# A macaron block (FFN, attention, FFN): the FFNs' down products by one level of Strassen's scheme, with sums on GpSimd and a new order of steps

## The chip, the cores and the metric

The kernel runs on one core of one Trainium2 chip. The metric is the device time of one execution in microseconds (us). Engines are named as in the profile: PE is TensorE (PEld its weight loads), DVE is VectorE, ACT is ScalarE, POOL is GpSimd, SP is SyncE, which issues most DMAs. Each engine works through its own queue in program order; semaphores carry what one engine needs of another.

## What is computed

Eight samples of 512 tokens with 256 channels pass through three residual branches. All of it is float32.

```python
x = x + 0.5 * ffn(layernorm(x))      # f1
x = x + attention(layernorm(x))      # at: 16 heads, causal, 32 wide
x = x + 0.5 * ffn(layernorm(x))      # f2, same weights as f1
def ffn(x):
    h = butterfly(x @ W_exp + b_exp, up_weights)     # 256 -> 1024, ten stages
    h = gelu(h + up_bias)
    return butterfly(h, down_weights) @ W_con + b_con + down_bias   # 1024 -> 256
```

The butterflies are linear, so the kernel folds each into its dense matrix once, at the start: an up matrix of 256 x 1024 (`wup_sb`) and a down matrix of 1024 x 256 (`wdn_sb`). The down product of one FFN of one sample is then a matrix of 512 x 1024 (gelu's output `g`) times one of 1024 x 256. There are sixteen of them.

## The kernel before

**The fold** (lines 719 to 742) builds the two matrices on all engines. For the down matrix, `high_stage` runs three times; its half on POOL is line 250, its sums on DVE are line 253. Between the stages the gelu steps of the first sample's f1 are issued. `low_down` (lines 342 to 346) finishes with eight products on PE (line 345) and eight copies on ACT into `wdn_sb` (line 346). After it stand the bias that `ffn_bias` (line 200, POOL) adds to x, and the layernorm of the next sample's f1.

**The steps.** Everything else is cut into steps of about 1.7 us on PE, and `ORDER` (lines 636 to 669) writes out by hand, sample by sample, in which order they are issued to all the queues. A token is a count, a letter and a distance to the sample that is meant. `f` and `g` are up steps of f1 and f2 (line 378): 128 of the 1024 hidden features for all 512 tokens, then gelu on ACT (line 392). `F` and `G` are down steps (line 396). `q`, `v`, `w` are the attention's projections. `u0` to `u9` are score units: products into the four banks `sc` (line 492), mask and maximum on DVE (line 506), exponentials on ACT (line 519). `t` transposes probabilities on DVE (line 537), `m` sends them across partitions by DMA (line 563), `p` multiplies them with v (line 576) and scales (line 583). `s`, `a`, `x` are a layernorm's statistics, application and transposition; the statistics use POOL for a power (line 169), the application is DVE's line 183, the transposition goes through DRAM by DMA except in three places.

**Products.** `product` (line 349) writes 128 output partitions as four matmuls of 32 columns of weights each, which run side by side in the array. In the profile each appears as two matmuls with two weight loads, as float32 needs two passes. I call the four that start together a burst.

**A down product** has eight steps: for each of four blocks of 128 tokens, twice four of the eight blocks of hidden features. Weights are 32 columns of `g`, and the 256 channels of `wdn_sb` are streamed:

```python
for fc in range(half * NBLK // 2, (half + 1) * NBLK // 2):
    product(py[:, i, :], lhsT=g[:, fc, bass.ts(t, P)], rhs=wdn_sb[:, fc, :],
            start=(fc == 0), stop=(fc == NBLK - 1))
```

Two token blocks share one bank of PSUM, and one DVE instruction adds them to x (line 414). For f2 SP then writes them to DRAM (line 416). In the last sample each block is added and written alone.

**Memory of PSUM.** Three banks (`ps_a`) turn over among up, down and projection products; four hold `sc`; one (`ps_o`) is for `p`.

Of the kernel before, what the change touches and what calls it, by code (L numbers as in the profile page):

```python
# [42 lines left out]
P = 128  # L43
# [5 lines left out]
def macaron_kernel(  # L49
# [64 lines left out]
    wdn_sb = const.tile([P, NBLK, C], F32, name="wdn_sb")  # L114

# [60 lines left out]
    def ln_apply(b, what, half, engine=nc.vector):  # L176
# [9 lines left out]
        if by_dma(b, what):  # L186
            if half == 0:
                kept["tx", what, b] = lnp.tile([P, 4, KC, NT, 32], F32, name=f"tx_{what}_{b}", tag="tx", bufs=2)
            for t in range(2):
                nc.vector.transpose(  # L190
                    kept["tx", what, b][:, :, :, 2 * half + t, :].rearrange("p j k r -> p k j r"),
                    xn[:, t, :].rearrange("p (k j s) -> p k j s", k=KC, j=4),
                )
# [94 lines left out]
    def first_ln_transposes():  # L288

        pts = [ps_f.tile([P, 512], F32, name=f"pxt_f1_0_{kc}", tag="f") for kc in range(KC)]  # L290
        xnt = kept["xnt", "f1", 0] = work.tile([P, 4, KC, P], F32, name="xnt_f1_0", tag="xnt", bufs=3)
# [57 lines left out]
    def product(out, lhsT, rhs, start, stop):  # L349

        for c in range(0, P, 32):
            nc.tensor.matmul(out[c : c + 32], lhsT=lhsT[:, c : c + 32], rhs=rhs, start=start, stop=stop)  # L352

    def ln_steps(b, what, **how):
        def new():
            kept["xnt", what, b] = work.tile([P, 4, KC, P], F32, name=f"xnt_{what}_{b}", tag="xnt", bufs=3)
            return kept["xnt", what, b]
# [19 lines left out]

    def up_steps(b, what):
        def step(fc):
            if fc == 0:  # L380
                kept["g", what, b] = work.tile([P, NBLK, N], F32, name=f"g_{what}_{b}", tag="g")
            g, xnt = kept["g", what, b], kept["xnt", what, b]
# [9 lines left out]
            nc.scalar.activation(g[:, fc, :], ph[:, :N], AF.Gelu, bias=bup_sb[:, fc : fc + 1])  # L392

        return [partial(step, fc) for fc in range(NBLK)]

    def down_steps(b, what, store):
        def step(t, half):
            t2, i = divmod(t, 2)

            n = 1 if store and b == B - 1 else 2  # L400
            if i % n == 0 and half == 0:
                kept["py", what, b] = ps_a.tile([P, 512], F32, name=f"py_{what}_{b}_{t // n}", tag="a")
            g, py = kept["g", what, b], kept["py", what, b].rearrange("p (t c) -> p t c", c=C)
            for fc in range(half * NBLK // 2, (half + 1) * NBLK // 2):
                product(
                    py[:, i, :],
                    lhsT=g[:, fc, bass.ts(t, P)],
                    rhs=wdn_sb[:, fc, :],
                    start=(fc == 0),
                    stop=(fc == NBLK - 1),  # L410
                )
            if (i + 1) % n == 0 and half == 1:
                mine = xt[b][:, t + 1 - n : t + 1, :]
                nc.vector.scalar_tensor_tensor(mine, py[:, i + 1 - n : i + 1, :], 0.5, mine, ALU.mult, ALU.add)  # L414
                if store:
                    nc.sync.dma_start(
                        out=out[b, bass.ds((t + 1 - n) * P, n * P), :].rearrange("(t p) c -> p t c", p=P), in_=mine
                    )

        return [partial(step, t, half) for t in range(NT) for half in range(2)]  # L420

    def qk_steps(b):
        def step(which, g):
            w, scale = ((wq_sb, QSCALE), (wk_sb, 1.0))[which]
            dst = work.tile([P, N], F32, name=f"{'qk'[which]}t_{b}_{g}", tag=f"{'qk'[which]}t", bufs=6)
# [139 lines left out]
    def times_v(b, g, pool):  # L565
# [4 lines left out]
        pa = ps_o.tile([P, 512], F32, name=f"pa_{b}_{g}", tag="pa")  # L570
# [46 lines left out]
    def attention_steps(b, pool):  # L617
        def moved(g):
            turn_sums(b, g)
            move(b, g, pool)  # L620

        return {
            "u": lambda n: score_unit(b, *UNITS[n], pool),
            "t": lambda n, part=0: turn(b, *UNITS[n], part, pool),
            "m": moved,
            "p": lambda g: times_v(b, g, pool),
        }

    ORDER = {
        0: """7F+0 x1+1 sa+0 aa+0 F+0 sa+0 x1+1 2f+1 aa+0 xa+0 f+1 xa+0 f+1 s1+2 2q+0 f+1 s1+2 u0 a1+2 2q+0 u1 v
              q+0 v t0 t1b u2 v 2f+1 t1a f+1 t2a m0 a1+2 u3 t2b 2F+1 u4 x1+2 t3 2F+1 t4b sa+1 v x1+2 q+0 t4a F+1
              u5 p0 m1 t5 u6 3F+1 aa+1 sa+1 2q+0 u7 f+2 t6b aa+1 t6a f+2 xa+1 f+2 xa+1 u8 t7a p1 2f+2 m2 2f+2 t8
              f+2 q+1 t7b q+1 u9 q+1 t9a t9b 2q+1 p2 m3""",  # L640
        1: """u0 F+1 q+0 u1 2F+1 t0 u2 F+1 t1b 2q+0 t1a u3 t2a p-3 m0 u4 2w-1 s2-1 a2-1 w-1 v w-1 s2-1 v t2b a2-1
              F+1 u5 v t3 x2-1 sa+1 3F+1 t4b v x2-1 aa+1 u6 p0 2g-1 sa+1 s1+2 aa+1 t4a xa+1 m1 g-1 a1+2 t5 g-1
              s1+2 4g-1 G-1 u7 xa+1 G-1 a1+2 x1+2 t7a x1+2 4G-1 t6a t6b u8 p1 m2 u9 t8 2G-1 f+2 q+1 f+2 t7b t9b
              f+2 q+1 f+2 t9a f+2 q+1 p2 f+2 m3""",
        2: """u0 2q+0 u1 t0 q+0 2f+1 u2 2q+0 t1a u3 p-3 t2a t1b u4 m0 2w-1 F+1 t2b u5 F+1 t3 F+1 t4a w-1 t4b F+1
              l+2 s2-1 w-1 2v s2-1 v 2a2-1 v F+1 sa+1 x2-1 F+1 u6 p0 F+1 t6a x2-1 m1 F+1 t6b t5 aa+1 sa+1 aa+1
              xa+1 7g-1 u7 s1+2 g-1 G-1 u8 t7a p1 t7b xa+1 m2 a1+2 u9 2G-1 q+1 G-1 s1+2 a1+2 t8 t9b 3G-1 x1+2 G-1
              t9a q+1 x1+2 2q+1 p2 m3""",
        3: """u0 2q+0 l+2 f+1 t0 4f+1 u1 2f+1 u2 p-3 w-1 t1b w-1 s2-1 q+0 t2a t1a u3 t2b m0 v 2w-1 v u4 t3 q+0
              a2-1 v f+1 u5 s2-1 a2-1 t4b v t4a 4F+1 u6 p0 x2-1 F+1 x2-1 m1 sa+1 2F+1 s1+2 u7 F+1 sa+1 aa+1 4g-1  # L650
              t7a aa+1 t5 t6a 2g-1 t6b xa+1 u8 p1 g-1 xa+1 g-1 m2 t7b u9 q+1 s1+2 q+1 a1+2 G-1 t9a a1+2 x1+2 t8
              t9b 2G-1 q+1 x1+2 G-1 q+1 p2 m3""",
        4: """u0 3G-2 t0 q+0 u1 G-2 q+0 u2 t1b 2f+1 q+0 t1a u3 p-3 l+2 u4 w-1 t3 v w-1 f+1 t2a w-1 s2-1 m0 v w-1
              t4b s2-1 2f+1 t2b 2a2-1 q+0 f+1 v x2-1 f+1 2s1+2 f+1 2F+1 v u5 p0 u6 x2-1 F+1 t4a F+1 m1 F+1 u7 t6a
              3F+1 g-1 sa+1 t5 2g-1 aa+1 sa+1 aa+1 g-1 t7a 2g-1 t6b u8 p1 2xa+1 g-1 m2 a1+2 g-1 t8 G-1 u9 2G-1
              a1+2 q+1 t7b G-1 2x1+2 t9a 2q+1 G-1 q+1 t9b p2 m3""",
        5: """u0 3G-2 u1 q+0 t0 2q+0 u2 f+1 t1b 2f+1 t1a u3 p-3 u4 w-1 t2a v t2b w-1 s2-1 q+0 l+2 m0 f+1 s1+2 v t3
              v t4a f+1 u5 t4b a2-1 w-1 f+1 w-1 f+1 s2-1 a2-1 v x2-1 f+1 s1+2 F+1 u6 p0 x2-1 m1 t6b 2F+1 a1+2 u7
              3F+1 t5 a1+2 F+1 sa+1 F+1 g-1 t7a x1+2 sa+1 g-1 aa+1 2g-1 aa+1 u8 t6a xa+1 p1 xa+1 4g-1 m2 x1+2 u9
              t9b t8 2q+1 2G-1 q+1 G-1 t9a t7b G-1 p2 m3""",  # L660
        6: """u0 q+0 2G-2 u1 G-2 q+0 u2 G-2 t1a t1b 2f+1 t0 t2a 2f+1 u3 p-3 m0 u4 w-1 t2b w-1 v 2w-1 v s2-1 q+0 v
              t4b t4a v t3 s2-1 f+1 u5 p0 m1 2f+1 a2-1 t5 f+1 u6 q+0 a2-1 F+1 t6b q+0 F+1 u7 F+1 t6a F+1 x2-1 t7a
              p1 x2-1 t7b m2 u8 sa+1 3F+1 u9 F+1 2g-1 sa+1 aa+1 g-1 aa+1 g-1 xa+1 t9a g-1 t8 g-1 t9b p2 xa+1 2g-1
              2q+1 m3""",
        7: """q+0 u0 q+0 u1 2G-2 t0 u2 p-3 t1a w-1 t1b t2a G-2 m0 u3 w-1 G-2 s2-1 u4 v t2b v t4a t3 2w-1 t4b v
              s2-1 v p0 m1 q+0 2a2-1 q+0 u5 q+0 u6 t5 G-2 q+0 t6b u7 2x2-1 t6a G-2 t7a p1 m2 u8 2G-2 g-1 t8 2g-1
              u9 t9a 2g-1 l+1 g-1 t9b t7b p2 2g-1 2G-1 m3 3G-1 p3 2w+0 s2+0 2w+0 a2+0 s2+0 2G-1 a2+0 G-1 2x2+0 8g+0
              8G+0""",
    }
# [8 lines left out]
    def sequence(b, pool):  # L678
        for token in ORDER[b].split():
            times, rest = (int(token[0]), token[1:]) if token[0].isdigit() else (1, token)  # L680
            what, kind, at = rest[0], "", 0
            if what in "sax":
                kind, rest = rest[1], rest[1:]
            if what in "ut":
                part = "ab".find(rest[-1])
                n = int(rest[1]) if part >= 0 else int(rest[1:])
            elif len(rest) > 1:
                at = int(rest[1:])
            for _ in range(times):
                if what == "u":  # L690
                    attention_steps(b, pool)["u"](n)
                elif what == "t":
                    attention_steps(b, pool)["t"](n, max(part, 0))
                elif what == "m":
                    attention_steps(b, pool)["m"](at)
                elif what == "p":
# [143 lines left out]
```

## Time and profile before

| what | us |
|---|---|
| median of 3 runs | 872.11 (870.77 to 872.52) |
| the profiled execution | 870.19 |
| its span in the profile | 868.2 |
| PE busy in it | 847.7 |
| DVE, ACT, POOL busy | 629.4, 517.8, 92.2 |
| granted TensorE clock | 1.00 in every stretch |

The span runs from the first to the last instruction; 2.0 us of the execution lie around it. A group's row in the profile gives its line, engine and operation, output and inputs, shape and count, then its busy time and the mean duration of one instruction, then the idle time of the engine in front of it and what ended that. Matmuls overlap in the pipeline: the mean duration of one is several times what it adds to a stream.

### The profile page before, as it was taken

The page shows a single profiled execution, that of the slowest core. Times are in us where ns is not written, and L with a number is a line of the kernel's source. Part 1 is how long each engine was busy: PE and PEld are TensorE (multiplying, and loading weights), DVE is VectorE, ACT ScalarE, POOL GpSimd, SP SyncE. Part 2 cuts the span into 40 slices and gives each one's busy share as a digit, 9 for nine tenths or more (in the row PEclk, how much of TensorE's full clock was granted, in tenths as well). Part 3 has the DMA queues.
Part 4 walks back from the last instruction along what each step waited for, and adds up shares of the span by engine and source line. Part 5 has one row for each costly group of instructions (what it writes and reads, how often), then busy time and mean ns, then how long its engine had stood idle before and what let it go on. Part 6 is the DMA issues. An engine that isn't in the chain of part 4 may idle for free.

```text
span 868.2 us, 28463 instructions
## 1 busy us (share of the span) xinstructions
PE 847.7 (98%) x11914; PEld 370.1 (43%) x11914; DVE 629.4 (73%) x1815; ACT 517.8 (60%) x1359; POOL 92.2 (11%) x123
## 2 busy tenths in 40 slices
PE   8999999999999999999999999999999999989898
PEld 7443524444334443443443434335344343433454
DVE  7948985997579685699777585888567794977430
ACT  6618686654585474776585654865746764747210
POOL 6511000011001010010102010021000100010010
PEclk9999999999999999999999999999999999999999
DMA  9210766637656568267765277557684577367400
GB/s 334 70 50 18 206 183 153 159 110 204 179 135 159 146 175 225 54 178 189 195 172 135 83 192 193 134 140 202 166 188 123 127 190 200 99 174 198 129 14 26
DMA packets 52832, 130.41 MB, mean 150 GB/s; under 512 B 10849, under 2 KB 32609, under 8 KB 52705
## 3 DMA queue, kind: packets, MB, share of 16 engines
q1 hardware_dynamic: 52560, 128.57, 55.8%
q8 instruction: 94, 1.54, 0.8%
q14 instruction: 34, 0.27, 0.1%
q10 hardware_dynamic: 144, 0.02, 0.0%
HBM read 21.80 MB, written 15.20 MB: 43 GB/s over the span
## 4 chain that ended last, share of the span: by engine, by line
PE 80%; SPq 5%; DVE 5%; DMA 4%; ACT 3%; issue 1%; DVEq 0%; ACTq 0%
PE ph_f L352 22%; PE py_f L352 22%; PE pp L352 11%; PE sc L492 8%; PE po L352 6%; PE pv L352 6%; SPq L563 5%; PE pa L576 5%; DVE e L506 3%; DMA out_dram<-x 1%; ACT e L519 1%; DMA pt<-pr 1%; DVE pr L537 1%; DMA wexp_sb<-in_wexp_t_dram 1%; DMA x<-in_x_dram 1%
## 5 line engine op out<-in xcount | busy, mean ns | idle before, releaser
L519 ACT ACTIVATE e<-e,nm 128x128 f32<-128x128 f32 (+3 forms) x512 | 280.4, 549 | 93.6 <-DVE nm L506 93.2
L506 DVE CUSTOM_DVE_ANT_0 e<-sc,mask 128x384 f32<-128x384 f32 (+2 forms) x384 | 196.4, 552 | 98.4 <-PE sc L492 97.8
L352 PE MATMUL py_f<-wdn_sb,g_f 128*32 128x256 f32 x4096 | 232.4, 380 | 0.0
L352 PE MATMUL ph_f<-xnt_f,wup_sb 128*32 128x512 f32 x2048 | 228.6, 593 | 0.6 <-ACT g_f L392 0.3
L537 DVE STREAM_TRANSPOSE pr<-e 128x1536 f32<-128x1536 f32 (+2 forms) x128 | 171.2, 1356 | 19.8 <-ACT e L519 19.8
L352 PEld LDWEIGHTS py_f<-wdn_sb,g_f 128*32 128x32 f32 x4096 | 131.9, 110 | 100.2 <-issue 19.3
L392 ACT ACTIVATE g_f<-ph_f,bup_sb 128x512 f32<-128x512 f32 x128 | 84.7, 686 | 90.6 <-PE ph_f L352 90.1
L352 PEld LDWEIGHTS ph_f<-xnt_f,wup_sb 128*32 128x32 f32 x2048 | 65.2, 110 | 139.7 <-issue 113.7
L519 ACT ACTIVATION_READ_ACCUMULATOR e<-e,nm 128x1 f32 x512 | 96.0, 188 | 0.0
L492 PE MATMUL sc<-kt,qt 32*64 32x512 f32 (+5 forms) x2048 | 86.6, 431 | 6.9 <-DVE nm L506 4.9
L576 PE MATMUL pa<-pt,v 128*32 128x512 f32 (+3 forms) x1024 | 75.4, 435 | 5.3 <-DMA pt<-pr 3.5
L169 POOL TENSOR_TENSOR rstd_f<-mv_f,mhalf 128x2 f32<-128x2 f32 x32 | 22.4, 702 | 481.6 <-DVE mv_f L167 463.2
L492 PEld LDWEIGHTS sc<-kt,qt 32*64 32x64 f32 x2048 | 40.8, 130 | 61.2 <-issue 27.3
L352 PE MATMUL pp<-xnt_at,wq_sb 128*32 128x512 f32 x512 | 61.0, 594 | 0.0
L352 PE MATMUL pp<-xnt_at,wk_sb 128*32 128x512 f32 x512 | 61.0, 593 | 0.0
L352 PE MATMUL po<-wo_sb,ot 128*32 128x256 f32 x1024 | 59.7, 380 | 0.4 <-DVE ot L583 0.4
L352 PE MATMUL pv<-wv_sb,xnt_at 128*32 128x512 f32 x512 | 59.7, 593 | 0.0
L576 PEld LDWEIGHTS pa<-pt,v 128*32 128x32 f32 x1024 | 31.8, 109 | 60.6 <-issue 50.1
L414 DVE SCALAR_TENSOR_TENSOR x<-py_f,x 128x512 f32<-128x512 f32 (+1 forms) x34 | 22.1, 649 | 44.4 <-PE py_f L352 44.4
L200 POOL TENSOR_TENSOR x<-x,bhalf 128x512 f32<-128x512 f32 x32 | 41.0, 1283 | 120.4 <-DVE xn_f L183 117.4
L519 ACT ACT_TABLE_LOAD x28 | 35.9, 1283 | 23.9 <-DVE nm L506 23.7
L583 DVE TENSOR_TENSOR ot<-pa,pt 128x512 f32<-128x512 f32 x32 | 21.8, 680 | 35.8 <-PE pa L576 35.8
(89 smaller groups left out, 577.3 us busy)
## 6 DMA issues: line engine op xcount, KB each, us to landing
pt<-pr SPq DMA_DIRECT2D x508, 176.0 KB, 4.3
td_f<-tx_f SPq DMA_DIRECT2D x14, 512.0 KB, 4.5
xnt_f<-td_f SPq DMA_DIRECT2D x56, 128.0 KB, 2.9
x<-in_x_dram SPq DMA_DIRECT2D x8, 512.0 KB, 6.1
td_at<-tx_at SPq DMA_DIRECT2D x7, 512.0 KB, 2.6
xnt_at<-td_at SPq DMA_DIRECT2D x28, 128.0 KB, 3.0
out_dram<-x SPq DMA_DIRECT2D x14, 256.0 KB, 4.2
wexp_sb<-in_wexp_t_dram SPq DMA_DIRECT2D x2, 514.0 KB, 7.7
```

What stands on the lines that cost most here:

```text
L169: nc.gpsimd.tensor_tensor(rstd, mv[:, :, 1], mhalf, ALU.pow)
L200: nc.gpsimd.tensor_tensor(x2, x2, bhalf.rearrange("p (o c) -> p o c", o=1).to_broadcast([P, 2, C]), ALU.add)
L352: nc.tensor.matmul(out[c : c + 32], lhsT=lhsT[:, c : c + 32], rhs=rhs, start=start, stop=stop)
L392: nc.scalar.activation(g[:, fc, :], ph[:, :N], AF.Gelu, bias=bup_sb[:, fc : fc + 1])
L414: nc.vector.scalar_tensor_tensor(mine, py[:, i + 1 - n : i + 1, :], 0.5, mine, ALU.mult, ALU.add)
L492: nc.tensor.matmul(sc[s : s + ROWS, j, at + low : at + high], lhsT=kept["q", b, gg][r, bass.ds(qb * P + s, ROWS)], rhs=kept["k", b, gg][r, ...
L506: nc.vector.tensor_tensor_reduce(out=e[:, j, at : at + n], in0=sc[:, j, at : at + n], in1=mask[:, N - n :] if qb else mask_first, scale=-1 ...
L519: nc.scalar.activation(e[:, j, at : at + n], e[:, j, at : at + n], AF.Exp, scale=-1.0, bias=nm[:, qb, gg, j : j + 1], accum_out=zs[:, gg, ...
L537: nc.vector.transpose(pr[:, :, :, qb : qb + 3 * n - 2 : 3, :].rearrange("p j h k r -> p h k j r"), blocks[:, :, :n])
L563: nc.sync.dma_start(out=pt[bass.ts(j, 32), i], in_=pr[bass.ts(i, 32), j])
L576: nc.tensor.matmul(by_row[r, :, kb * 32 :], lhsT=v[:, kb, bass.ds(g * P + j * HD, HD)], rhs=pt[:, :, bass.ds(j * NSLOT + SLOT[kb] + kb, NT ...
L583: nc.vector.tensor_tensor(kept["ot", b][:, g, :].rearrange("p (i q r) -> p i q r", i=4, r=32), pa.rearrange("p (i q r) -> p i q r", i=4, r ...
```

## The change

The down product is cut into quarters, and seven products of quarters take the place of eight. Write the gelu output as a11, a12 (the first 256 tokens, with hidden features 0 to 511 and 512 to 1023), a21 and a22 (the other 256 tokens), and the down matrix as b11, b12, b21, b22 (hidden halves by channel halves). Weight sums are made once, in the fold, by four DVE instructions. Sums of `g` are made for every FFN on POOL, mostly in place. Seven steps k0 to k6 each multiply one pair and add the result to one or two quarters of x; since running sums stay in PSUM, the bank `u` collects k0, k3, k5 and k6, the bank `q` collects k2 and k4, and `r` holds k1. A step now has two token blocks times four feature blocks, and streams 128 channels per matmul.

```diff
+    wmix_sb = const.tile([P, 3, NBLK // 2, C // 2], F32, name="wmix_sb")
...
-                kept["tx", what, b] = lnp.tile([P, 4, KC, NT, 32], F32, name=f"tx_{what}_{b}", tag="tx", bufs=2)
+                kept["tx", what, b] = lnp.tile([P, 4, KC, NT, 32], F32, name=f"tx_{what}_{b}", tag="tx", bufs=1)
...
+    def mix_weights():
+        nc.vector.tensor_tensor(t1, b12, b11, ALU.subtract)
+        nc.vector.tensor_tensor(t2, b22, t1, ALU.subtract)
+        nc.vector.tensor_tensor(t4, b21, t2, ALU.subtract)
+        nc.vector.tensor_tensor(b12, b22, b12, ALU.subtract)
...
     def up_steps(b, what):
-        def step(fc):
+        def step(n):
+            pair, second = divmod(n, 2)
+            fc = pair + HALF * second
...
+            if second:
+                a11, a21, a22 = g[:, pair, EARLY], g[:, pair, LATE], g[:, fc, LATE]
+                nc.gpsimd.tensor_tensor(kept["s1", what, b][:, pair], a21, a22, ALU.add)
+                nc.gpsimd.tensor_tensor(a21, a11, a21, ALU.subtract)
...
+        def half_product(out, a, w, start):
+            for t in range(2):
+                for f in range(HALF):
+                    product(
+                        out[:, t, :],
+                        lhsT=a[:, f, bass.ts(t, P)],
+                        rhs=w[:, f, :],
+                        start=start and f == 0,
+                        stop=f == HALF - 1,
+                    )
...
+        def add(m, n, part, tokens=slice(0, 2)):
+            mine = quarter(m, n)[:, tokens]
+            nc.vector.scalar_tensor_tensor(mine, part[:, tokens], 0.5, mine, ALU.mult, ALU.add)
...
+            if k == 0:
+                kept["pu", what, b] = bank("u", ps_y, "y")
+                u = kept["pu", what, b][:, 0]
+                half_product(u, a11, w11, True)
+                for f in (slice(0, HALF // 2), slice(HALF // 2, HALF)):
+                    nc.gpsimd.tensor_tensor(a11[:, f], s1[:, f], a11[:, f], ALU.subtract)
+                add(0, 0, u)
+                return
...
+            if k == 1:
+                r = bank("r", ps_a, "a")[:, 0]
+                half_product(r, a12, w21, True)
+                for f in (slice(0, HALF // 2), slice(HALF // 2, HALF)):
+                    nc.gpsimd.tensor_tensor(a12[:, f], a12[:, f], a11[:, f], ALU.subtract)
+                add(0, 0, r)
+            elif k == 2:
+                kept["pq", what, b] = bank("q", ps_a, "a")[:, 0]
+                half_product(kept["pq", what, b], s1, t1, True)
+                add(1, 1, kept["pq", what, b])
+            elif k == 3:
+                half_product(u, a11, t2, False)
+                add(0, 1, u)
+            elif k == 4:
+                half_product(kept["pq", what, b], a12, w22, False)
+                add(0, 1, kept["pq", what, b])
+                put(0)
+            elif k == 5:
+                half_product(u, a21, t3, False)
+                add(1, 1, u)
+            else:
+                half_product(u, a22, t4, False)
+                add(1, 0, u)
+                put(1)
...
-        pa = ps_o.tile([P, 512], F32, name=f"pa_{b}_{g}", tag="pa")
+        pa = ps_a.tile([P, 512], F32, name=f"pa_{b}_{g}", tag="a")
...
         low_down(mats, cur)
+        mix_weights()
         run(partial(ffn_bias, 0, 0), partial(ffn_bias, 0, 1))
         run(lns(1, "f1"))
...
+    STEPS = """
+        2x1@1 5F@0 sa@0 F@0 aa@0 F@0 sa@0 2f@1 aa@0 2xa@0 s1@2 2q@0 f@1 u0@0 q@0 s1@2 t0a@0 a1@2 2f@1 q@0 u1@0
+        2v@0 a1@2 t1b@0 q@0 u2@0 t1a@0 3f@1 t2a@0 m0@0 u3@0 t2b@0 2F@1 u4@0 t3a@0 q@0 2F@1 v@0 t4a@0 2x1@2 u5@0
+        F@1 v@0 sa@1 t4b@0 p0@0 m1@0 u6@0 F@1 aa@1 t5a@0 2q@0 t6a@0 t6b@0 F@1 sa@1 2f@2 u7@0 2f@2 aa@1 u8@0 p1@0
+        2f@2 2xa@1 t7a@0 m2@0 f@2 u9@0 t8a@0 2q@1 t7b@0 t9a@0 f@2 F@2 q@1 u0@1 q@1 t9b@0 p2@0 m3@0 u1@1 F@2
...
+        xa@6 t7b@5 3g@4 m2@5 2g@4 G@4 u9@5 G@4 t8a@5 t9b@5 t9a@5 2q@6 2G@4 x1@7 q@6 p2@5 m3@5 G@4 u0@6 q@6 G@4
+        u1@6 G@4 t0a@6 2f@7 q@6 u2@6 t1b@6 f@7 p3@5 t2a@6 t1a@6 m0@6 2w@5 u3@6 t2b@6 v@6 q@6 u4@6 t4a@6 f@7 v@6
+        2w@5 u5@6 2v@6 t3a@6 t4b@6 p0@6 m1@6 t5a@6 3f@7 2s2@5 a2@5 f@7 u6@6 a2@5 2x2@5 2q@6 t6a@6 2F@7 t6b@6
...
+        w@6 s2@6 t3a@7 v@7 t4b@7 q@7 s2@6 2a2@6 t4a@7 2v@7 x2@6 v@7 p0@7 m1@7 u5@7 x2@6 q@7 G@5 u6@7 t5a@7 t6b@7
+        2G@5 q@7 u7@7 G@5 t6a@7 t7a@7 p1@7 m2@7 u8@7 G@5 t8a@7 5g@6 t7b@7 u9@7 g@6 t9a@7 g@6 t9b@7 p2@7 m3@7 g@6
+    """
```

`mix_weights` overwrites b12 with its difference from b22 (t3). The bank of `ps_o` becomes `ps_y` and holds `u`; `p` now takes a bank of `ps_a`. Up steps run in the order 0, 4, 1, 5, 2, 6, 3, 7, and after each second one POOL makes that pair's two sums. `STEPS` replaces `ORDER`: one list for all samples, in which the sample stands after `@`; steps f, g, q, v, w, u, t, m, p and the layernorms' are as numerous as before, F and G are seven per FFN. Of the list, the first four lines, three from late in it and the last two are shown. Three tags get fewer buffers: `tx` 1 in place of 2, `xnt` 2 in place of 3, `qt` and `kt` 5 in place of 6.

## The prediction

> **What bounds the kernel now.** I read the page's busy times first, then its chain of work that ended last.
>
> ```profile
> span 868.2 us, 28463 instructions
> PE 847.7 (98%) x11914; PEld 370.1 (43%) x11914; DVE 629.4 (73%) x1815; ACT 517.8 (60%) x1359; POOL 92.2 (11%) x123
> PE 80%; SPq 5%; DVE 5%; DMA 4%; ACT 3%; issue 1%; DVEq 0%; ACTq 0%
> ```
>
> PE is busy nearly throughout and is 80% of the chain. A busy PE proves little, as ends are modelled, so the waits on PE come next, together with those of its weight loads.
>
> ```profile
> PEld sc L492 <- DVE nm L506: 15.5, 19, 1.7
> PE sc L492 <- DVE nm L506: 4.9, 10, 0.8
> PE pa L576 <- DMA pt<-pr: 3.5, 2, 2.0
> ```
>
> The columns are us in total, times, longest. PE waits for little: 5 to 16 us on the score banks, 3.5 us on a transfer. So the length of PE's stream is the time, and what the change takes from that stream counts in full unless a new wait appears. Last I read groups with shapes kept apart, for prices.
>
> ```profile
> L352 PE MATMUL py_f<-wdn_sb,g_f 128*32 128x256 f32 x4096 | 232.4, 380 | 0.0
> L576 PE MATMUL pa<-pt,v 128*32 128x512 f32 x256 | 33.9, 601 | 5.3 <-DMA pt<-pr 3.5 <-DMA out_dram<-x 1.5 <-issue 0.3
> L576 PE MATMUL pa<-pt,v 128*32 128x256 f32 x256 | 19.8, 379 | 0.0
> L576 PE MATMUL pa<-pt,v 128*32 128x128 f32 x256 | 13.0, 273 | 0.0
> L329 PE MATMUL pup<-ident,high_up 128*128 128x128 f32 x8 | 1.0, 272 | 0.0
> L414 DVE SCALAR_TENSOR_TENSOR x<-py_f,x 128x512 f32<-128x512 f32 x30 | 20.4, 679 | 18.3 <-PE py_f L352 18.3
> L414 DVE SCALAR_TENSOR_TENSOR x<-py_f,x 128x256 f32<-128x256 f32 x4 | 1.7, 425 | 26.1 <-PE py_f L352 26.1
> L200 POOL TENSOR_TENSOR x<-x,bhalf 128x512 f32<-128x512 f32 x32 | 41.0, 1283 | 120.4 <-DVE xn_f L183 117.4 <-DVE bhalf L739 3.0
> ```
>
> **1. The products themselves.** In the chain's pieces 32 `py` matmuls, eight bursts, take 1.73 us: 0.216 us a burst of 256 columns, 13.8 us for the 64 bursts of a down product. After the change there are 7 steps x 2 token blocks x 4 feature blocks x 2 passes = 112 bursts of 128 columns. What does one cost? The `pa` rows have the same four-way form at several widths. Each call of `p` has two bursts per width, so 33.9, 19.8 and 13.0 over 32 calls are 1.059, 0.619 and 0.406 us; less the mean of one matmul, 0.458, 0.240 and 0.133 remain from first to last start. From 256 to 128 columns that falls by 0.107, so a burst of 128 costs 0.216 - 0.107 = 0.109. These bursts are only two in a row. A stream of 128-column matmuls, each with its own weight load, is at `pup`: 8 on line 329 span 1.04 us in the timeline, (1.04 - 0.272) / 7 = 0.110; on line 316, with one slow start included, 30 span 3.62 us, (3.62 - 0.275) / 29 = 0.115. I take 0.111, near the plain stream: 112 x 0.111 = 12.4 us, a gain of 1.4 us per down product (0.9 at 0.115, 1.6 at 0.109). For the fourteen products between the first and the last: -19 us (-13 to -22).
>
> [...]
>
> **2. The first product, in the fold.** Here the price is in the queues, so I read the timeline of the first 60 us (start, length).
>
> ```profile
> 30.91 2.82 POOL L250 TENSOR_SCALAR mine_dn<-high_dn,dnc_sb 128x256 f32<-128x256 f32 x4 [1.15 <-DVE high_dn L253]
> 34.93 3.42 ACT L346 COPY wdn_sb<-low_dn 128x256 f32<-128x256 f32 x8
> 36.56 0.42 DVE L165 BATCH_NORM_STATS2 st_f<-x 128x6 f32<-128x256 f32 x1
> 42.59 1.28 POOL L200 TENSOR_TENSOR x<-x,bhalf 128x512 f32<-128x512 f32 x1 [0.55 <-DVE xn_f L183]
> 51.71 3.62 PE L352 MATMUL ph_f<-xnt_f,wup_sb 128*32 128x512 f32 x32
> ```
>
> The down product runs from 37.9 to 51.7, and DVE and POOL do the next sample's layernorm beside it. `mix_weights` is put ahead of that layernorm in DVE's queue. Its second subtraction needs the last copy of `wdn_sb`, at 38.35; three of 0.69 (L235, 512 elements) follow to 40.5, and as line 253, which also has two inputs in SBUF, goes up to 698 ns beside POOL and takes 471 at least, I say 41. So the layernorm begins 4.5 us later, and its last bias addition on POOL ends at 43.9 + 4.5 = 48.4. POOL's update of a11 after k0 is queued behind that addition, and DVE's add of k0 is behind the layernorm too: both hold k3, which PE could start at 37.9 + 5.3 = 43.2. The update is two instructions of 1.28: done at 51.0. k3 then lacks six of its eight block products, 1.3 us; the update of a12 is done at 53.5, k4 ends at 54.9, k5 at 56.6, k6, after 0.65 for the add in between, at 59.1. PE has no other step to do until then, so the up step that began at 51.7 begins at 59.1: +7.4 us. Next, `2xa@0` is followed at once by q, without the up step that used to cover a copy of 0.69: +0.5. POOL's L250 at 30.9 waits behind two pair sums for about 2 us, but the eight products of `low_down` leave room. Together +8 (from -1, if all hides, to +10).
>
> **3. The other products.** k3 needs two updates of a11 after k0, 2.6 us of POOL, and k4 two more, 5.1 us. Counted in `STEPS`, PE has at least 3.5 and 5.3 us of other steps in between, so nothing is lost (if a POOL instruction took half longer, as one group of L250 does against the other, 719 and 480 ns for one shape, the three products with the least in between would lose about 2.4 us each: +7). k6 adds onto the bank that the add after k5 must have read: 0.43 plus two hand-overs, about 0.65. Seven products have 2.7 us or more of other steps there; seven have only one score unit, about 1 us, which covers the add if DVE is free. DVE is busy three quarters of the time, so I take 0.3 for each, +2 (from 0 to 7 x 1.76 = +12, if a whole transposition of 1.76, L537, stands ahead every time).
>
> **4. The last product.** Nothing lies beside it. Steps take 7 x 1.78 + 0.65 = 13.1 against 13.9, updates are in time by the 3.5 and 5.3 us again; the last transfer is 256 KB in place of 128 KB, median landing 4.2 against 1.7 us in a loaded and an idle queue, of which I charge 0.5. Together -0.4 (-1 to +2).
>
> **5. The order.** In `ORDER` 11 of the distances between score units have under 3 us of matmuls in between, in `STEPS` one. A unit's `sc` is free only after 3.1 to 4.0 us of DVE (four or eight of L506), so waits on the score banks should shrink: I take -4, near the 4.9 of PE's own row (-15 to +6, since each other distance is new too).
>
> **6. Off the path.** DVE: seven adds of 0.425 for two of 0.68, +1.6 x 16 = 26, plus mixing 2.8. L183's application has minimum, median and maximum 371, 407 and 1019 ns; one of 0.91 us at 41.29 in the timeline stands beside a POOL addition that began at 40.76:
>
> ```profile
> L183 DVE TENSOR_SCALAR xn_f<-x,mv_f,rstd_f x60: 371/407/1019, 39.9 to 834.4; 128x256 f32<-128x256 f32 x60
> ```
>
> With POOL at 30% that is 92 x 0.2 x 0.55 = 10 us. DVE ends near 670 of 855, 78%: still below PE. POOL gains 16 x (8 x 0.64 + 4 x 1.28) = 164 us, ending near 256. ACT changes between gelu and exponential 64 times for 56: 8 loads of 1.28, 10 us. If this cover were gone, PE would wait at `sc`, which step 5's upper end holds.
>
> [...]
>
> **Sum.** -19 + 8 + 2 - 0.4 - 4 = -13.4 on a span of 868.2: 854.8. The profiled execution was 2.0 longer than its span, and the median 1.9 above that execution, so 858.7, say 859.
>
> **Rivals.**
> - *The first product hides too, or the order gives more.* Then +8 becomes about 0: 851, or 846 with the order at -9. For it: the waits on `sc` sum to 20 if the rows for loads and matmuls are added. Against: POOL's queue is in order, and the additions stand ahead of the updates. 0.18.
> - *The accumulating bank decides, and it is slower.* One place: `u`, read by an add in DVE's queue before k3, k5 and k6 may go on. Price: a transposition of 1.76 ahead of the add in each of fourteen products, at k5 or k6, 24.6 in place of 2: 881. It decides from about 0.95 us of waiting per product (13.4 / 14). For it: DVE at 78%, in order. Against: in seven products 2.7 us or more lie between. 0.13.
> - *Half the width is not half the time.* If bursts cost 0.133, the start-to-start figure of `pa` not freed of its stagger, a product takes 14.9, +1.1 x 16 in place of -19 and the tail's gain: 896. From 0.123 (13.8 / 112) the products gain nothing. Against: lines 329 and 316. 0.05.
> - *About no change*, when two of these meet halfway: 0.05.
>
> **Chances.** Forecast 0.59 (852 to 868). Faster by over 0.2%, about what a measurement of this kernel can tell from no change: 0.59 + 0.18 = 0.77; within it 0.05; slower 0.18. The range 846 to 877 leaves out the far part of the slower cases and the best of the first rival.
>
> **What would show it.** Right: `py` groups with 7168 matmuls, about 200 us busy in place of 232; in the first product a gap of PE before k3 ended by POOL, and the first sample-1 up step near 59; POOL near 256, DVE near 670; the last product about 13 us. Wrong: PE waits ended by DVE's add or by POOL in later products (rival two), or a burst spacing above 0.12 in an unbroken run of steps (rival three); or no gap before k3.

## The result, and the profile after

The changed kernel takes 875.25 us in the median (871.76 to 878.44, 10 runs) against 870.94 (870.63 to 872.52, 10 runs): a ratio of 1.0048, 95% interval 1.0031 to 1.0065. It is slower by about 4.3 us where I forecast 12 less. Its own runs also spread more than those of the kernel before. The profiled execution took 876.94, with a span of 875.1.

The page of the changed kernel: the span, the busy times, the clock granted to PE in 40 slices of 21.9 us, the chain of work that ended last.

```profile
span 875.1 us, 34994 instructions
PE 833.6 (95%) x14986; PEld 439.8 (50%) x14986; DVE 673.5 (77%) x1897; ACT 527.0 (60%) x1367; POOL 268.6 (31%) x315
PEclk9989999999999999999999999999999999998999
PE 67%; DVE 13%; ACT 9%; issue 3%; SPq 3%; DMA 2%; POOL 1%; DVEq 0%; ACTq 0%; POOLq 0%
```

PE has 14 us less to do than before (833.6 for 847.7), and yet the span is 7 longer. In the chain PE falls from 80% to 67%, DVE rises from 5 to 13 and ACT from 3 to 9: PE now waits. What it waits for is in the waits of the changed kernel (us in total, times, longest):

```profile
PE pyq_f L353 <- DVE x L450: 5.5, 1, 5.5
PE pa L655 <- DMA xnt_f<-td_f: 5.0, 1, 5.0
PE ph_f L353 <- ACT g_f L419: 2.5, 2, 1.4
PE pyu_f L353 <- ACT g_f L419: 2.4, 3, 0.8
PE pyr_f L353 <- ACT g_f L419: 2.2, 1, 2.2
```

The waits on score banks, which led the list before, have shrunk as I said (2.1 us for 4.9). New ones stand ahead of them: one long wait in the first product, a `p` that waits for a transfer, and eight waits for gelu of 8.3 us together, of which the kernel before had one:

```profile
PE ph_f L352 <- ACT g_f L392: 0.3, 1, 0.3
```

The groups of `py` have 7168 matmuls, 16 products of 112 bursts, and start to start of every fourth is 109 ns from the first quartile to the third: a burst of 128 columns costs half of one of 256 (216 ns). In the timeline below, k1 and k2 begin 1.75 us apart, sixteen bursts. So the products do what they say, and the loss must lie between them. The timeline of the first product shows the longest wait (start, length):

```profile
43.29 1.93 PE L353 MATMUL pyr_f<-wdn_sb,g_f 128*32 128x128 f32 x64
...
44.72 3.40 POOL L470 TENSOR_TENSOR g_f<-gs_f,g_f 128x512 f32<-128x512 f32 x2
...
45.04 1.93 PE L353 MATMUL pyq_f<-wmix_sb,gs_f 128*32 128x128 f32 x64
45.23 1.76 DVE L397 TENSOR_TENSOR wdn_sb<-wdn_sb 128x512 f32<-128x512 f32 x1
...
47.80 1.96 PE L353 MATMUL pyu_f<-wmix_sb,g_f 128*32 128x128 f32 x64 [0.83 <-DVE x L450]
...
54.74 0.38 DVE L450 SCALAR_TENSOR_TENSOR x<-pyq_f,x 128x256 f32<-128x256 f32 x1
...
55.27 3.64 PE L353 MATMUL pyq_f<-wdn_sb,g_f 128*32 128x128 f32 x64 [5.51 <-DVE x L450]
...
63.88 2.33 PE L353 MATMUL ph_f<-xnt_f,wup_sb 128*32 128x512 f32 x20
```

k4 adds onto the bank q, so it waits until DVE has added k2's sum to x. That addition is in DVE's queue behind the mixing of the weights (line 397 is its last instruction) and the next sample's layernorm, and comes 8 us after k2 has ended. k4 itself then takes 3.64 in place of 1.9, at a granted clock of 0.50 (1.00 until 53.7). k3 (47.80) was held for 0.83 only, and by DVE's addition of k0: POOL's update of a11 (line 470) ends at 48.12, while k3 runs. The first up step of sample 1 begins at 63.88; before it was 51.71, and I had said 59.1.

### The profile page after: what moved, and what is told of

Same layout as the page of the kernel before. It is cut to its first block, busy times and chain, and to the rows that moved or that the text cites. A ratio compares the mean times of both kernels' runs of the same rounds, so it can differ in the third digit from the quotient of the medians.

```text
span 875.1 us, 34994 instructions
## 1 busy us (share of the span) xinstructions
PE 833.6 (95%) x14986; PEld 439.8 (50%) x14986; DVE 673.5 (77%) x1897; ACT 527.0 (60%) x1367; POOL 268.6 (31%) x315
## 4 chain that ended last, share of the span: by engine, by line
PE 67%; DVE 13%; ACT 9%; issue 3%; SPq 3%; DMA 2%; POOL 1%; DVEq 0%; ACTq 0%; POOLq 0%
PE ph_f L353 16%; PE pp L353 11%; PE pyu_f L353 10%; PE sc L571 7%; PE pyq_f L353 6%; PE pa L655 6%; ACT e L598 5%; PE po L353 5%; PE pv L353 4%; PE pyr_f L353 3%; DVE pr L616 2%; SPq L642 2%; DVE e L585 2%; ACT L598 1%; ACT L419 1%
## 5 line engine op out<-in xcount | busy, mean ns | idle before, releaser
L422 POOL TENSOR_TENSOR gs_f<-g_f 128x256 f32<-128x256 f32 x64 | 47.8, 747 | 305.9 <-ACT g_f L419 303.4
L353 PEld LDWEIGHTS ph_f<-xnt_f,wup_sb 128*32 128x32 f32 x2048 | 67.2, 110 | 139.3 <-issue 113.0
L655 PE MATMUL pa<-pt,v 128*32 128x512 f32 (+3 forms) x1024 | 77.5, 442 | 6.8 <-DMA xnt_f<-td_f 5.0
L353 PE MATMUL pyu_f<-wdn_sb,g_f 128*32 128x128 f32 x2048 | 64.0, 276 | 2.5 <-ACT g_f L419 2.4
L353 PE MATMUL pyu_f<-wmix_sb,g_f 128*32 128x128 f32 x2048 | 63.0, 273 | 3.4 <-DVE x L450 1.9
L353 PEld LDWEIGHTS pyu_f<-wdn_sb,g_f 128*32 128x32 f32 x2048 | 56.6, 111 | 14.3 <-issue 9.5
L655 PEld LDWEIGHTS pa<-pt,v 128*32 128x32 f32 x1024 | 34.6, 112 | 57.9 <-issue 45.4
L353 PEld LDWEIGHTS pyu_f<-wmix_sb,g_f 128*32 128x32 f32 x2048 | 55.6, 110 | 12.9 <-issue 6.6
```

Of the source, the lines that this page charges most:

```text
L422: nc.gpsimd.tensor_tensor(kept["s1", what, b][:, pair], a21, a22, ALU.add)
L655: nc.tensor.matmul(by_row[r, :, kb * 32 :], lhsT=v[:, kb, bass.ds(g * P + j * HD, HD)], rhs=pt[:, :, bass.ds(j * NSLOT + SLOT[kb] + kb, NT ...
```

## The experiments

Three theories stood at the start. **A**: the first product in the fold loses the time. **B**: the sums on POOL do, by holding DVE back in all products. **C**: the new list of steps costs time by itself. A fourth, **D**, came with the second group: that `p` now takes one of the three common banks. Times are medians; a difference is taken against the kernel before in the same group of runs (870.3 to 871.0).

### The first product

**e1_first_plain.** The first sample's f1 keeps its plain down product, has no sums, and the weight sums come later, when that product has ended.

```diff
+    def plain(b, what):
+        return (b, what) == (0, "f1")
+
     def down_steps(b, what, store):
+        if plain(b, what):
+            return plain_steps(b, what, store)
...
-        mix_weights()
         run(partial(ffn_bias, 0, 0), partial(ffn_bias, 0, 1))
...
-        2x1@1 5F@0 sa@0 F@0 aa@0 F@0 sa@0 2f@1 aa@0 2xa@0 s1@2 2q@0 f@1 u0@0
+        2x1@1 5F@0 sa@0 F@0 aa@0 F@0 sa@0 2f@1 aa@0 2xa@0 s1@2 2q@0 M@0 f@1 u0@0
```

> Edit: the first sample's f1 keeps the plain down product (eight half steps in its seven places), its pair sums on POOL are left out, and the weight sums are made after it instead of ahead of the next layernorm; the other fifteen products stay as in the changed kernel. Theory A (the first product in the fold cost what the other products gained: its own product runs from 41.5 to 63.9 where the kernel before has 37.9 to 51.7): the stretch returns to 37.9 to 51.7, the clock stays at 1.00 there, and the time falls by about 12 us, to 863. Theory B (POOL's sums hold DVE back all through the kernel, the first product is only one of sixteen): about 4 us less, 871. Theory C (the new order costs what the products gain): also about 12 less, it isn't told apart here.

Measured: 865.18 (861.19 to 869.33), ratio 0.994 (0.9919 to 0.9962). It beats both kernels. Against before it stands at -5.4, the changed kernel at +4.3: the first product, with the weight sums ahead of the layernorm, costs 9.7 us. In its timeline the up step and the third weight sum stand like this:

```profile
51.08 3.62 PE L353 MATMUL ph_f<-xnt_f,wup_sb 128*32 128x512 f32 x32
```
```profile
59.39 0.69 DVE L396 TENSOR_TENSOR wmix_sb<-wdn_sb,wmix_sb 128x512 f32<-128x512 f32 x1
```

The up step is back at the time of before. The same weight sum, with no POOL instruction beside it, takes 0.69; in the changed kernel it took 1.66, beside a bias addition and an update of a11 on POOL. A holds, but the remaining 5.4 are still 12 us short of the 17.4 that fifteen products should give (steps 1, 3 and 4).

**e7_mix_in_place.** As e1, with `mix_weights` left ahead of the layernorm. Its first product then reads the difference t3 in the place of b12, and so must wait for the last weight sum.

```diff
-2q@0 M@0 f@1 u0@0
+2q@0 f@1 u0@0
...
         low_down(mats, cur)
+        mix_weights()
```

> The changed kernel with a plain first down product and no sums for it, but with the four weight sums left where the change has them, ahead of the layernorm in DVE's queue. With the weight sums moved behind two q steps it took 865. If the first product's own chain of updates and additions costs the head's 10 us: 865 to 867. If the place of the weight sums does: 870 to 875.

Measured: 870.99 (866.36 to 873.87), ratio 0.9998 (0.9982 to 1.0014). It doesn't tell the two apart as I meant it to: the 3.55 us that PE waits at 37.6 are for that weight sum, a dependence which the edit made. The first up step comes 5.5 later than in e1 (56.62), and the median is 5.4 above e1's, as if a delay at the head passed on in full. But the profiled executions of the two, with the same delay, took 866.36 and 864.28, only 2.1 apart, so how much passes on isn't shown.

### The sums on POOL

**e3_no_sums** takes all of POOL's sums out of the changed kernel, **e8_plain_no_sums** out of e1.

```diff
-                nc.gpsimd.tensor_tensor(kept["s1", what, b][:, pair], a21, a22, ALU.add)
-                nc.gpsimd.tensor_tensor(a21, a11, a21, ALU.subtract)
...
-                half_product(kept["pq", what, b], s1, t1, True)
+                half_product(kept["pq", what, b], a22, t1, True)
```

> Edit: the changed kernel without any sum of gelu's output on POOL (half products take the plain quarters of g, so the products are not those of the scheme); weight sums, adds and order stay. Theory A: the fold's down matrix is ready at the old time and the mixing on DVE meets less of POOL, so about 7 us of the first product's loss go, and some 3 us of waits for sums in the others: 865. Theory B: 15 us or more go, 860 or less, with DVE's busy time back near 650. Theory C: at most 7 less, 868 or more.

> The kernel with the plain first product (weight sums behind two q steps) without any sum of gelu's output on POOL: s1 is replaced by a22, and a11, a21, a12 stay as gelu left them, so the fifteen products are not those of the scheme. If POOL's sums cost only beside the first product: 863 to 866, as with them. If they also cost beside the other fifteen (locked DVE, late updates; theory B): 855 to 860.

Measured: e3 865.73 (863.5 to 867.14), ratio 0.9953 (0.9937 to 0.9968); e8 862.21 (859.57 to 862.82), ratio 0.9891 (0.9873 to 0.991). With the first product plain, the sums of the other fifteen cost 3.3 us (8.7 less than before, for 5.4); the other 5.8 of the 9.1 that e3 saves belong, by difference, to the first product, where theory A has them already. B is a small term, below what I expected of it.

### The list of steps

**e2_order_alone** is the changed kernel with plain products everywhere; **e5_order_own_bank** gives `p` its own bank again; **e6_before_shared_bank** is the kernel before with `p` in a common bank; **e13_list_alone** is e5 with the buffers and the sequence of up steps of before, so that the list is all that differs.

```diff
# e2
+    def plain(b, what):
+        return True
+
     def down_steps(b, what, store):
+        if plain(b, what):
+            return plain_steps(b, what, store)
...
# e5: and
-        pa = ps_a.tile([P, 512], F32, name=f"pa_{b}_{g}", tag="a")
+        pa = ps_y.tile([P, 512], F32, name=f"pa_{b}_{g}", tag="y")
...
# e13: and
-            pair, second = divmod(n, 2)
-            fc = pair + HALF * second
+            fc = n
...
-name=f"tx_{what}_{b}", tag="tx", bufs=1
+name=f"tx_{what}_{b}", tag="tx", bufs=2
-name=f"xnt_{what}_{b}", tag="xnt", bufs=2
+name=f"xnt_{what}_{b}", tag="xnt", bufs=3
-tag=f"{'qk'[which]}t", bufs=5
+tag=f"{'qk'[which]}t", bufs=6
...
# e6, from the kernel before
-        pa = ps_o.tile([P, 512], F32, name=f"pa_{b}_{g}", tag="pa")
+        pa = ps_a.tile([P, 512], F32, name=f"pa_{b}_{g}", tag="a")
```

> Edit: the new order with plain down products everywhere (eight half steps in seven places, the last place has two), no pair sums, no weight sums, no sums in place. What is left of the change is the order, the smaller buffers and the bank of p. Theory A: the order is worth little, within 4 us of the kernel before, 867 to 875. Theory B: the same, as nothing is left on POOL. Theory C: 880 or more, as the fifteen products then take 1.4 us more each and the order's waits stay.

> The new order, the up steps in their new sequence and the fewer buffers, with plain down products everywhere (no sums, no weight sums), and the attention's p in a bank of its own as before, so that PSUM is divided as in the kernel before. The run with p among the three common banks took 886. If the order of steps costs the time (theory C): 881 to 886, with PE's waits for gelu, qt and the transposition's DMA still there. If the shared bank costs it (theory D): 868 to 873.

> The kernel before, with one edit: p takes one of the three common banks, and the fourth is left unused. Theory C (the order costs the 15 us): 871 to 873. Theory D (the bank does): 880 to 886.

> The new list of steps and nothing else of the change: plain products, p's bank of its own, the buffers (tx 2, xnt 3, qt and kt 6) and the sequence of up steps as in the kernel before. With fewer buffers and the new sequence it took 882. If the list costs the 11 us: 880 to 884. If the fewer buffers or the up sequence do: 870 to 874.

| kernel | us | ratio to before |
|---|---|---|
| e2 | 886.11 | 1.018 (1.0164 to 1.0196) |
| e5 | 882.08 | 1.0124 (1.0109 to 1.0139) |
| e6 | 876.43 | 1.0059 (1.0044 to 1.0074) |
| e13 | 882.6 | 1.0132 (1.0111 to 1.0152) |

C holds: the list costs 11.8 us, and the buffers and the up sequence nothing that shows (e5, 11.1). Some 0.8 of this is not the list: the plain products here write the last sample in pairs of blocks, and its last product takes 18.4 us to the end of the span, for 17.5 before. A shared bank costs 5.5 where `py` holds a common bank through four steps (e6). What `p`'s place costs beside the new products, where the long-lived sum u is in another bank, was not run; it is part of the next term. As a chain of runs, each less the one before it, so that the terms add up by construction, the ledger reads: list, from before to e5, +11.1. Fifteen products with their sums, banks and weight sums, from e5 to e1, -16.5. First product, from e1 to the changed kernel, +9.7. Sum +4.3.

### By what the list costs

The waits of PE in e13 name ACT:

```profile
PE py_f L352 <- ACT g_f L403: 2.7, 3, 1.6
PE pp L352 <- ACT g_f L403: 2.5, 2, 1.8
PE py_f L352 <- ACT qt L526: 2.4, 2, 1.6
```

with the smaller ones 9.7 in all; the kernel before had 2.4. One such place in its timeline, ACT and PE:

```profile
129.73 0.18 ACT L608 ACTIVATION_READ_ACCUMULATOR e<-e,nm 128x1 f32 x1
129.93 1.28 ACT L403 ACT_TABLE_LOAD   x1
...
131.23 1.85 ACT L403 ACTIVATE g_f<-ph_f,bup_sb 128x512 f32<-128x512 f32 x3
...
131.97 1.92 PE L352 MATMUL pp<-xnt_at,wq_sb 128*32 128x512 f32 x16 [1.83 <-ACT g_f L403]
...
133.09 1.28 ACT L608 ACT_TABLE_LOAD   x1
```

A score unit's exponentials hold ACT until 129.9. Then ACT loads gelu's table for 1.28, runs three gelus that PE's banks have been waiting for, and loads the other table at once, since the next unit is due. PE's next projection waits 1.83 for a bank that gelu has yet to read.

**e16_before_one_table**, **e17_list_one_table** and **e18_plain_one_table** put the exponential in the place of gelu in the kernel before, in e13 and in e1. The trace of each then has one table load, at the start, where the kernel before has 57 more and the other two have 65 more. The edit is one word:

```diff
-            nc.scalar.activation(g[:, fc, :], ph[:, :N], AF.Gelu, bias=bup_sb[:, fc : fc + 1])
+            nc.scalar.activation(g[:, fc, :], ph[:, :N], AF.Exp, bias=bup_sb[:, fc : fc + 1])
```

> The kernel before with the exponential in the place of gelu, so that ACT has one table of functions and its table loads (57 of 1.28 us) go; the output is not the reference's. PE's waits for ACT were 2.4 us in all: 867 to 871 (871 with the loads).

> The new list alone (plain products, buffers as before; 883) with the exponential in the place of gelu, so that ACT's 65 table loads go; the output is not the reference's. If the list costs its 12 us through ACT (steps of exponentials and gelus nearer to each other, more table loads, PE's 9 us of waits for ACT's results): 870 to 874, within 4 of e16_before_one_table. If it costs them through the moves and the other waits: 878 to 882.

> The new list with the plain first product (865) and the exponential in the place of gelu; the output is not the reference's. If what the list still loses here is ACT's: 853 to 858. If it is p's moves and POOL's and DVE's sums: 861 to 865.

| kernel | with two tables | with one | ratio of the latter to before |
|---|---|---|---|
| before | 870.85 | 870.12 | 0.9986 (0.9973 to 0.9998) |
| list alone (e13) | 882.6 | 870.08 | 0.9994 (0.9981 to 1.0007) |
| e1 | 865.18 | 853.09 | 0.9793 (0.9769 to 0.9816) |

The loads are the only thing that the edit takes out, as ACT needs as long for either function (687 and 685 ns in the mean). The row of gelu's table loads in e13, then gelu's row in e13 and its row in e17, where it is the exponential:

```profile
L403 ACT ACT_TABLE_LOAD x33 | 42.3, 1283 | 6.9 <-PE ph_f L352 6.4
L403 ACT ACTIVATE g_f<-ph_f,bup_sb 128x512 f32<-128x512 f32 x128 | 86.1, 687 | 104.4 <-PE ph_f L352 103.5 <-POOL mine_dn L250 0.6
L403 ACT ACTIVATE g_f<-ph_f,bup_sb 128x512 f32<-128x512 f32 x128 | 87.2, 685 | 138.4 <-PE ph_f L352 137.7 <-POOL mine_dn L250 0.6
```

Without table loads the two lists take the same time, so the whole cost of the list runs through them. The old list loses under 1 us by its 57 loads, the new one 12.5 by its 65: what counts is not 65 x 1.28 us of ACT but which of them PE waits for. In e17 PE's waits for ACT are down from 9.7 to 0.9 us, this line and one of 0.2:

```profile
PE sc L581 <- ACT kt L526: 0.7, 1, 0.7
```

e1 loses the same 12, so the cost is there under the new products too, and with one table the fifteen products are worth 17.0 (870.08 to 853.09), as above. The number of loads and their place weren't varied apart.

In the timeline above the last exponential's read-out ends at 129.91, the load runs from 129.93, and gelu starts at 131.23: from function to function this switch took 1.32 us, 1.28 of it the load.

### The old list under the new products

If the list costs 11 us, the old one should be better. **e9_old_steps** is e1 with the old list (one F or G token less per product), **e12_old_steps_all** the changed kernel with it. **e10_q_beside_u**, made from e9, lays q into the unused half of u's bank; **e11_last_apart**, made from e10, besides gives k6 a sum of its own. **e14_last_apart** does the latter in e1, with a common bank.

```diff
# e9, e12: STEPS holds ORDER's tokens, for example
-        2x1@1 5F@0 sa@0 F@0 aa@0 F@0 sa@0 2f@1 aa@0 2xa@0 s1@2 2q@0
+        7F@0 x1@1 sa@0 aa@0 F@0 sa@0 x1@1 2f@1 aa@0 xa@0 f@1 xa@0 f@1 s1@2 2q@0
...
# e10: and
-                kept["pq", what, b] = bank("q", ps_a, "a")[:, 0]
+                kept["pq", what, b] = kept["pu", what, b][:, 1]
...
# e11: and (e14 with bank("l", ps_a, "a")[:, 0] for kept["pq", what, b])
                 add(1, 1, u)
+                add(1, 0, u)
             else:
-                half_product(u, a22, t4, False)
-                add(1, 0, u)
+                half_product(kept["pq", what, b], a22, t4, True)
+                add(1, 0, kept["pq", what, b])
```

> The kernel with the plain first product (weight sums behind two q steps; 865 with the new list of steps), with the list of the kernel before in the place of the new one: of each product's eight F or G tokens the last is left out, the first product keeps eight. The fewer buffers and the new sequence of up steps stay. If the order of steps costs the 11 us that the runs with plain products gave (theory C): 852 to 857. If the fewer buffers or the up sequence cost them: 863 to 867.

> The changed kernel, its first product and weight sums in the fold included, with the list of steps of the kernel before (the last of each product's eight F or G tokens left out). Theory C (the order costs 11): 862 to 866. If what the order costs and what the first product costs are the same waits at the head: 868 to 873. If the order is not the cause: 874 to 877.

> As e9_old_steps, and the sum q lies in the unused half of u's bank, so that the three common banks hold q no longer. If the common banks are short since p takes one of them (5 us with plain products): 2 to 5 us less than e9_old_steps. If that shortage has gone with py, which held a common bank through four steps: the same within 1.

> As e10_q_beside_u, and k6 no longer collects on u behind k5: after k5 DVE adds u to both quarters of the late tokens, and k6 starts a sum of its own in q's half, added to its quarter. This takes the wait for the addition after k5 away and adds one DVE instruction of 0.41 to each product. If those waits (0.7 to 1.07 each where nothing lies between) cost PE: 5 to 12 us less than e10_q_beside_u. If other work fills them: within 2 of it.

> The new list with the plain first product (865), and k6 in a bank of its own among the common three: DVE adds u to both late quarters after k5, and k6's sum to its quarter. If the wait of k6 for the addition after k5 costs PE (stalls from pyu to pyu, 5.2 us over 8 places): 859 to 862. If the common banks are short, so that the wait comes back as one for a bank: 864 to 869.

| kernel | us | ratio to before |
|---|---|---|
| e9 | 922.86 | 1.0617 (1.0588 to 1.0646) |
| e12 | 943.54 | 1.0839 (1.0816 to 1.0861) |
| e10 | 959.93 | 1.1034 (1.1016 to 1.1051) |
| e11 | 966.76 | 1.1108 (1.1084 to 1.1132) |
| e14 | 865.74 | 0.9935 (0.9918 to 0.9953) |

I was wrong in all but the last. The terms don't add: the old list is 58 us worse under the new products (e9 against e1), and the new one, 11 us worse under the old products, is the better one here. One wait of PE in e9, and its timeline at one such place, PE and DVE:

```profile
PE pyu_f L353 <- DVE x L455: 25.8, 13, 3.9
```
```profile
335.74 1.96 PE L353 MATMUL pyu_f<-wdn_sb,g_f 128*32 128x128 f32 x64
...
337.62 1.74 DVE L646 STREAM_TRANSPOSE pr<-e 128x1536 f32<-128x1536 f32 x1
...
340.77 0.41 DVE L455 SCALAR_TENSOR_TENSOR x<-pyu_f,x 128x256 f32<-128x256 f32 x1
341.23 1.95 PE L353 MATMUL pyu_f<-wmix_sb,g_f 128*32 128x128 f32 x64 [3.53 <-DVE x L455]
```

k5 is done at 337.7. Its addition stands in DVE's queue behind a layernorm's application and three transpositions and comes at 340.8; k6, which adds onto the same bank, waits 3.5 us. The old list sets steps of a product next to each other where the new one puts score units and projections between them. In e9 the additions on u and q account for 31 us of waiting, against 0.5 in e1; the two profiles differ by 55 in span, and the rest (longer waits for ACT among it, 17.5 for 10.3) isn't split. This is my rival of the accumulating bank, priced at 24.6, in a list that I hadn't considered. With the first product and its weight sums as in the changed kernel (e12) another 20.7 us come on top, where the new list had 9.7.

e10 makes it worse: with q in u's bank PE waits for additions for 64.5 us.

```profile
PE pyu_f L353 <- DVE x L455: 64.5, 40, 5.8
```

These are forty waits in place of e9's fifteen (thirteen on u, two of 5.3 us on q). The row doesn't tell which sum's addition ended a wait; that a step also waits for additions of the other sum in its bank is my reading, and wasn't tested by itself. e11, which takes k6 off the sum of k5 but leaves both sums in one bank, gains nothing: its waits for those additions are 67.4 us.

e14 shows that in the new list the wait for k5's addition costs nothing that can be measured: the same as e1 within the intervals.

### Half clock, and the last sample's transfers

The windows view of the changed kernel gives span, busy times, granted clock, DMA share and GB/s; here around two of the three places where the clock falls.

```profile
50.00:62.00 12.00, 6.29 (x128) 6.05 (x128) 7.52 (x19) 0.00 (x0) 5.62 (x6) 0.72 0.27 89
785.00:797.00 12.00, 7.05 (x112) 3.23 (x108) 6.78 (x19) 3.21 (x14) 0.00 (x0) 0.72 0.48 116
```

**e4_clock_held** puts matmuls that nobody reads into both waits: six products ahead of k4 of the first product, five ahead of the last sample's `p1`.

```diff
+            if what == "D":
+                filler = ps_a.tile([P, 512], F32, name=f"filler_{c}", tag="a")
+                for _ in range(6 if c == 0 else 5):
+                    product(filler, lhsT=wup_sb[:, 0, :P], rhs=wup_sb[:, 1, :512], start=True, stop=True)
...
-        2x1@1 5F@0 sa@0
+        2x1@1 4F@0 D@0 F@0 sa@0
...
-p1@7 m2@7
+D@7 p1@7 m2@7
```

**e15_two_queues** is e1 with half of the last sample's moves issued by GpSimd.

```diff
-                nc.sync.dma_start(out=pt[bass.ts(j, 32), i], in_=pr[bass.ts(i, 32), j])
+                queue = nc.gpsimd if b == B - 1 and d >= 2 else nc.sync
+                queue.dma_start(out=pt[bass.ts(j, 32), i], in_=pr[bass.ts(i, 32), j])
```

> Edit: the changed kernel with matmuls that nothing reads where PE waited longest: about 5 us of them ahead of the fifth step of the first product (PE waited 5.5 us there) and about 4 us ahead of p1 of the last sample (5.0 us). They keep PE busy in waits that stay as long as before. If the granted clock of a half after these waits (6.8 us each in the profile) costs time, the clock stays at 1.00 there and 3 to 5 us go: 871. If it doesn't, the time stays at 875 or rises by what of the filling isn't covered.

> The new list with the plain first product (865), and half of the last sample's moves issued by GpSimd instead of SyncE, so that sixteen moves need not 11 us to be issued. If p's waits in the last sample (4.1 and, behind gelu, 2.3, with 6.8 and 3.4 us of half clock after them) are time: 858 to 862. If the chain behind them takes it back: 864 to 866. If GpSimd's issuing delays its sums of gelu's output: above 866.

Measured: e4 872.76 (870.45 to 876.19), ratio 1.002 (1.0003 to 1.0038), with the clock at 1.00 in both stretches: 2.1 us less than the changed kernel, though the intervals overlap slightly. e15 867.35 (864.0 to 867.93), ratio 0.9957 (0.9941 to 0.9974): `p`'s waits for transfers fall from 4.1 to 0.5 us, and the time is no less than e1's. In the profile others are longer than in e1: at k4 of an f2 product PE stands for 2.4 us with nothing shown to wait for, and k1's wait for gelu is 2.2 for 1.1. Whether these are the same time come back wasn't tested.

## Why the prediction was wrong

The failing step is the fifth, together with the sixth. In the terms of the ledger:

| term | predicted | measured |
|---|---|---|
| list (steps 5 and 6) | -4 | +11.1 |
| fifteen products (steps 1, 3, 4) | -17.4 | -16.5 |
| first product (step 2) | +8 | +9.7 |
| sum | -13.4 | +4.3 |

- **Step 1 was right.** A burst costs 0.109 us where I took 0.111; the price of half width not being half time didn't appear. By 0.109 the fourteen products gain 22, not 19.
- **Step 2 came near its size by another path**, so the nearness is in part luck. I had POOL's update of a11 hold k3; k3 waited only 0.8 us, for DVE's addition of k0. I overlooked k4's own hold, the addition of k2 on q, which cost 5.5. The up step came 4.8 later than I said. I gave the eight products of `low_down` room that wasn't there: line 254 took 738 ns for 553 beside the pair sums, and the first product began at 41.52 for 37.87. The mixing took 5.7 us where I had 2.8. Against this the updates on POOL came earlier than I had them, ahead of the layernorm's powers.
- **Step 3** held in sum. The sums on POOL cost 3.3 where I took nothing (bound +7); k6's wait, which I took at 2, shows no price (e14). With step 1's 22 and step 4 this makes some -19; no run assigns the 3 us from there to -16.5.
- **Step 4** held: the last product takes 17.1 us to the end of the span, for 17.5. (Its own terms give -0.3, not -0.4.)
- **Step 5 failed.** I counted the distances between score units and looked at one wait, that of PE on `sc`. That wait did shrink, by 3 us, also in e13 (1.7 for 4.9). I didn't ask what the same moves do to ACT. Units nearer to up steps and projections put table loads and exponentials ahead of gelu, and PE waits for gelu's bank.
- **Step 6 failed** in one sentence: it counted the eight further loads (right, 65 for 57), called them off the path since ACT is busy 60%, and kept only `sc` as the place where they could show. They show at `ph`, `pp` and `py`, and e17 gives their price, 12.5 us.
- **The rivals.** The accumulating bank costs where the steps of a product are adjacent (e9); in the changed kernel the additions hold u for 1.9 us in all, and q for 5.5 in the first product alone. That the list could be a loss stood only in the range of step 5, whose upper end (+6) was too low; no rival gave it a mechanism.

The 9.7 us of the changed kernel's head aren't split further: in e7 the added dependence hides the answer, so the parts of mixing, k4's wait and half clock (2.1 with the one at `p1`) stay open. The split into three terms also holds for this chain of runs alone: by way of e9 it would be another.

## What to carry to other kernels

An order of steps written by hand serves every engine's queue at once: when it changes, count for each engine what now stands ahead of what PE needs next, above all the switches of ACT's tables, before giving the order a price. An engine that is busy 60% can still be late where PE needs it. And an order is priced only together with the work that it was made for: the new list stood at +11 us against the old under one kind of product and at -58 under the other.

## What the runs showed of the hardware

- The granted clock of PE is 0.50 in three stretches of the changed kernel, and 0.99 to 1.00 in the windows before, between and behind them: from 53.8 to 60.6 us, beginning in a wait of 5.5 that ends at 55.3; from 323.5 to 326.9, as a wait of 2.2 ends; from 787.7 to 794.5, beginning in one of 5.0 that ends at 790.4. In e1 the windows give 0.77 over 770 to 785 us and 0.83 over 798 to 808, which is about 6.9 and 3.4 us at a half; its waits there are of 3.9 and 2.3. In e15 three waits of PE last 2.2 to 2.4, while the mean clock of 0.996 over 861.8 us leaves about 7 us at a half. By my estimate from these numbers that is two stretches of 3.4 at most, one fewer than the waits, so the length of the wait alone doesn't seem to decide; what does was not tested. Nor is it shown that the half clock makes the times of a kernel spread: e10, with a mean clock of 0.973 where the changed kernel has 0.990, spreads by 2.3 us in four runs.
- In the first product of the changed kernel three of the four weight sums on DVE (512 elements) take 1.58, 1.66 and 1.76 us beside POOL's bias additions and updates of a11; the first takes 0.68, with POOL's addition beginning 0.17 after it. In e1 all four take 0.68 to 0.69, the last two with no POOL instruction beside them. On POOL the two bias additions there take 3.35 us together and the two updates 3.40, where the median of one is 1.28 and 1.29 over the kernel.
